# Moving one operand sum behind two masks, half of a normalising to VectorE, two loads ahead of three stores, and one bias step to a later slice

## The chip, the core and the metric

The kernel runs on one core of a Trainium2 chip. The core has five instruction queues that matter here: TensorE (PE; its weight loads are listed apart as PEld), VectorE (DVE), ScalarE (ACT), GpSimd (POOL) and SyncE (SP), which in this kernel only issues DMAs. Each queue runs its instructions strictly in the order in which they were written; queues wait for each other through semaphores. The metric is the device time of one execution in microseconds, as the median of several runs; less is better.

## The reference

`x` is 128 graphs of 128 nodes with 768 features, `adj` a weighted adjacency matrix for each graph, and there are 12 heads of 64 features. All numbers are float32.

```python
h = jnp.maximum(_layernorm(x, axis=-1), 0.0)
q, k, v = (_split_heads(h @ W + b) for W, b in ((Wq, bq), (Wk, bk), (Wv, bv)))
scores = jnp.einsum('bhqd,bhkd->bhqk', q, k) / jnp.sqrt(HD)
scores = scores + beta * adj_e
scores = jnp.where(adj_e > 0, scores, -9000000000000000.0)
out = jnp.einsum('bhqk,bhkd->bhqd', softmax(scores, axis=-1), v)
x = x + merge_heads(out)
```

## The kernel before

The 128 graphs are worked in 32 groups of four (G = 0 to 31). For each group the hidden rows `h` are turned so that features lie on the partitions (tiles A00 to A12), and three projections follow, called slices: "qk0" (heads 0 to 5 of Q and K), "v" (V), and "qk1" (heads 6 to 11 of Q and K). Behind every slice some of the attention is woven in: `scores` (Q against K on TensorE into a PSUM buffer), a mask (one VectorE instruction, line 637, which adds the bias and so frees that PSUM buffer), the exponential on ScalarE (line 639), and `attend` (line 686).

Group 0 is computed by `plain_slice`: ordinary tiled matmuls (line 845), 18 steps a slice. Groups 1 to 31 are computed by `slice_z`: a slice is 15 products (table PRODUCTS), each the matmul of a sum of activation tiles (S0 to S14, or an A tile itself) with a sum of weight tiles (T...). A product is 14 matmuls of line 550, which the profile counts as 28 because a float32 matmul has two records. The 15 products are spread over four chains a, b, c, d; the products of a chain add up in one PSUM buffer, and after each product VectorE (line 574) or ScalarE (lines 568 and 570, for the first use of an output tile) takes the buffer's present state into the output tiles (`home`). So a chain's next product waits for the eviction of its last one. There are four PSUM buffers in all (`pairs`), for chains, scores and attention together.

The order of the 15 products in a slice is written out: PORDER for "qk0" and "v", QORDER for "qk1", ZORDER for "qk0" of group 1 alone, LORDER for the last slice. I call the first product of a slice place 0 and the last place 14. In PORDER places 0 to 9 hold products 1, 0, 5, 2, 3, 10, 7, 6, 13, 11; their chains are a, c, a, c, b, a, b, c, a, b. In ZORDER product 7 stands at place 5.

What else is done at a place is hung into `todo`. `run` takes a product's matmuls, then the masks that are pending, then `todo[at]`, then what is overdue, then the product's evictions, then what trails, and then `todo[at, "post"]`. From the end of the first slice on this order is kept as written on every engine (`manual_schedule`).

- Activation sums are VectorE instructions of line 467 on 128x896 elements (`sum_acts`). In "qk0" S7 stands at place 0, S0 at 1, S5 at 5, S14 at 8, S11 at 9; for group 1 S6 stands ahead of S7. S7 is A01 - S10 and is read by product 7 and by the sum S14; S0 is read by product 10.
- At place 2 of "qk0" two scores are issued, so their masks (tiles e_5 and e_3) come behind the product at place 3. For group 1 these scores stand at places 3 and 5. A third score follows place 6.
- Most weight sums are kept in DRAM and streamed in (`load_T`, line 338; tile T_qk or T_v) into a ring of five buffers; 11 of the 45 stay resident. A product that used a streamed one issues the next load.
- The weight sums are made once, during group 0, by `prepare`: `sums` and `rest` (lines 303, 305, 282, 283 on VectorE, 285 to 288 on GpSimd) and a store to DRAM (`kept`, line 291). The steps are taken one or two at a place; the last stores and the first five loads of group 1 fall into group 0's "qk1" slice, the loads at places 10 to 14.
- Group 0's rows 2 and 3 of `x` are normalised in place: `moments_2` makes the scale (line 395) and the shift (line 397) on GpSimd, `norm` applies them in four ScalarE instructions a graph (line 449), and `to_hT` turns them on VectorE (line 462).
- `halve_bias` (line 977) is one GpSimd instruction that turns the V bias into the form that `slice_z` wants; it stands at place 1 of group 0's "qk1", and its result is first read in group 1's "v".

Of the kernel before, what the change touches and what calls it, by code (L numbers as in the profile page):

```python
# [14 lines left out]
ALU = mybir.AluOpType  # L15
# [4 lines left out]
GRP = 4  # L20
# [89 lines left out]
QORDER = (4, 0, 1, 8, 2, 3, 5, 6, 7, 10, 9, 11, 13, 12, 14)  # L110
LORDER = (1, 4, 0, 8, 5, 2, 10, 3, 6, 7, 13, 9, 11, 12, 14)
PORDER = (1, 0, 5, 2, 3, 10, 7, 6, 13, 11, 4, 9, 14, 8, 12)
ORDER = {"qk0": PORDER, "v": PORDER, "qk1": QORDER}
RING = 5
RESIDENT = (3, 8, 12, 16, 20, 25, 29, 33, 35, 38, 41)

# [10 lines left out]
def direct(ctx, tc, x, adj, wq, bq, wk, bk, wv, bv, beta, out, bad):  # L127
# [10 lines left out]
    nc = tc.nc  # L138
# [10 lines left out]
    NB = P // SQ  # L149
# [12 lines left out]
    xg, xp, A, full, wide, biasT, vt, qk = {}, {}, {}, {}, {}, {}, {}, {}  # L162
# [7 lines left out]
    def block(i):  # L170
        return flat(7 * P * i, 7 * P * (i + 1)).rearrange("p (z n) -> p z n", n=P)
# [22 lines left out]
    for g in range(2):  # L194
        t = xg[0, g]
# [64 lines left out]

    sequence = [(sl, n) for sl in ("qk0", "v", "qk1") for n in ORDER[sl]]
    resident = {key: const.tile([P, 7, P], F32, name=f"res_{key[0]}_{key[1]}") for key in (sequence[at] for at in RESIDENT)}
# [3 lines left out]
    def quarters(t):  # L266
        return t[:, 0:6].rearrange("p (c z) n -> p c z n", c=2)[:, :, 0:2]

    def prepare(sl):

        def home(name):
            n = [i for i, p in enumerate(PRODUCTS) if p[1] == name][0]
            if (sl, n) in resident:
                return resident[sl, n]
            made_in[0] += sl != "qk1"
            if sl != "qk1" and made_in[0] % 8 in (2, 5, 7):
                t = work.tile([P, 2, W], F32, tag="e", name=f"prep_{sl}_{n}", bufs=3)
                return t.rearrange("p i w -> p (i w)")[:, 0:7 * P].rearrange("p (z n) -> p z n", n=P)
            return work.tile([P, 7, P], F32, tag="T", name=f"prep_{sl}_{n}", bufs=RING)

        def rest(n, t, b11, b12, b22, b=None):
            nc.vector.tensor_tensor(t[:, 6], b12, b11, ALU.subtract)
            nc.vector.tensor_tensor(t[:, 2], b22, b12, ALU.add)
            if b is not None:
                nc.gpsimd.tensor_copy(t[:, 0:2], b[:, 0])
                nc.gpsimd.tensor_copy(t[:, 3], b[:, 1, 0])
            nc.gpsimd.tensor_tensor(t[:, 4], t[:, 1], t[:, 6], ALU.add)
            nc.gpsimd.tensor_tensor(t[:, 5], t[:, 0], t[:, 4], ALU.subtract)
            if (sl, n) not in resident:
                k = kept[sl, n] = dram.tile([P, 7, P], F32, name=f"kept_{sl}_{n}")  # L290
                nc.sync.dma_start(k, t)

        made = {}

        def sums(name):
            for out, a, b, sign in SUMS_B:
                if out == name:
                    if out not in made:
                        made[out] = home(out)
                    at = [quarters(made[q]) if q in made else wt[sl, q] for q in (a.strip("-"), b)]  # L300
                    op = ALU.add if sign > 0 else ALU.subtract
                    if a[0] == "-":
                        nc.vector.scalar_tensor_tensor(quarters(made[out]), at[0], -1.0, at[1], op0=ALU.mult, op1=op)
                    else:
                        nc.vector.tensor_tensor(quarters(made[out]), at[0], at[1], op)

        def finish(name):
            n = [i for i, p in enumerate(PRODUCTS) if p[1] == name][0]
            if name in made:
                t = made[name]  # L310
                rest(n, t, t[:, 3], t[:, 4], t[:, 1])
            else:
                t, b = home(name), wt[sl, name]
                rest(n, t, b[:, 1, 0], b[:, 1, 1], b[:, 0, 1], b)

        steps = []
        for first, then_finish in PREPARED:
            for name in first:
                steps.append(lambda name=name: sums(name))
            for name in then_finish:  # L320
                steps.append(lambda name=name: finish(name))
        return steps

    def order_of(G, sl):
        if G == 1 and sl == "qk0":
            return ZORDER
        return LORDER if G == NG - 1 and sl == "qk1" else ORDER[sl]

# [27 lines left out]
    st, pm, rstd, shift = {}, {}, {}, {}  # L356
# [88 lines left out]
    def norm(G, g, lo=0, hi=NB):  # L445
        for b in range(lo, hi):
            t = xg[G, g][:, b, :]
            n = g * NB + b
            nc.scalar.activation(t, t, AF.Relu, bias=shift[G, n], scale=rstd[G, n])  # L449

    def home_A(G, name):
        if (G, name) in wide:
# [11 lines left out]
    def sum_acts(G, name):  # L464
        _, a, b, sign = [row for row in SUMS_A if row[0] == name][0]
        t = full[G, name] = block(SPOT.index(name))
        nc.vector.tensor_tensor(t, full[G, a], full[G, b], ALU.add if sign > 0 else ALU.subtract)  # L467
# [411 lines left out]
    first = {}  # L879
# [71 lines left out]
    def half(step):  # L951

        if step == 0:
            for g in range(2, GRP):
                stats(0, g)
        elif step == 1:
            first["got"] = moments_1(0, 2 * NB, 4 * NB)
        else:
            first["pool"] = moments_2(0, 2 * NB, 4 * NB, *first["got"])
            for g in range(2, GRP):  # L960
                norm(0, g)
            for k in range(3):
                first["dve"] = to_hT(0, 1, k)

# [17 lines left out]
    todo, steps, mom = {}, {}, []  # L982

    def then(at, f, *args):
        todo.setdefault(at, []).append(lambda: f(*args))

    def bias(G, *at):
        def go():
            if G not in steps:
                steps[G] = bias_steps(G)  # L990
            next(steps[G], None)
        for n in at:
            then(n, go)
# [17 lines left out]
    def sums_at(G, slots):  # L1011
        for at, name in slots:
            then(at, sum_acts, G, name)
# [43 lines left out]
    turn_act(1, ((4, "A01"), (5, "A02"), (6, "A00"), (9, "A10"), (10, "A11"), (11, "A12")))  # L1057
    for n in range(18):
        then(n, step, 2 - (n > 8))
    then(1, halve_bias)  # L1060
    sums_at(1, ((12, "S1"), (13, "S9"), (14, "S10"), (15, "S2")))
    then(0, row_moments, 2)
    then((7, "post"), load_x, 2, 0)
    then((14, "post"), load_row, 3, 0)
    then(12, homes.append, block(len(SPOT)))
    bias(1, 4, 6, 8)
    for n in range(RING):
        then(10 + n, load_T)
    plain_slice(0, "qk1", todo, (1, 0))

    for G in range(1, NG):
        more = G + 1 < NG
        todo.clear()
        then(2 + (G == 1), scores, G - 1, 1, 2)
        then(2 + 3 * (G == 1), scores, G - 1, 1, 0)
        then((6, "post"), scores, G - 1, 1, 1)
        attention(G - 1, 1, ((7, 2), (10, 0), (12, 1)))
        sums_at(G, ((0, "S7"), (1, "S0"), (5, "S5"), (8, "S14"), (9, "S11")))
        if G == 1:
            todo[0].insert(0, lambda: sum_acts(1, "S6"))  # L1080
        if more:
            for n, at in enumerate((1, 2, 4, 5)):
                then((at, "post"), norm, G + 1, n // 2, n % 2 * 2, n % 2 * 2 + 2)
            turn_act(G + 1, ((8, "A01"), (9, "A00"), (11, "A02")), None)
            then((12, "post"), load_x, G + 1, 1)
            if G + 2 < NG:
                then((7, "post"), row_stats, G + 2, 0)
                then((9, "post"), load_row, G + 2, 1)
        slice_z(G, "qk0", todo)

        todo.clear()
        then(2, scores, G, 0, 2)
        then(2, scores, G, 0, 1)
        then(7, scores, G, 0, 0)
        if more:
            then((11, "post"), add_raw, G + 1)
            for n, at in enumerate((3, 4, 6, 7)):
                then((at, "post"), norm, G + 1, 2 + n // 2, n % 2 * 2, n % 2 * 2 + 2)
            turn_act(G + 1, ((10, "A11"),), 1)
            for at, name in ((4, "A01"), (5, "A00"), (6, "A02")):  # L1100
                then(at, inner, G + 1, name)
            if G + 2 < NG:
                for g, at in ((1, 1), (2, 5), (3, 10)):
                    then((at, "post"), row_stats, G + 2, g)
                    if g < 3:
                        then((at + 1, "post"), load_row, G + 2, g + 1)
        slice_z(G, "v", todo)

        todo.clear()
        if not more:  # L1110
            break
        attention(G, 0, ((3, 2), (9, 1)))
        attention(G, 0, ((12, 0),), 6)
        turn_act(G + 1, ((1, "A10"), (4, "A12")), 1)
        sums_at(G + 1, ((6, "S1"), (7, "S9"), (8, "S2"), (11, "S6"), (13, "S10")))
        bias(G + 1, 0, 2, 4)
        if G + 2 < NG:
            then(5, row_moments, G + 2, 6, 9)
            then((6, "post"), load_x, G + 2, 0)
        if G + 3 < NG:  # L1120
            then((10, "post"), load_row, G + 3, 0)
        slice_z(G, "qk1", todo)
# [158 lines left out]
```

## Time and profile before

| | |
|---|---|
| median of 3 runs | 2697.48 us (2691.35 to 2700.34) |
| the profiled execution's own time | 2692.31 us |
| its span, first to last instruction | 2690.5 us |
| mean granted TensorE clock | 0.997 |
| one middle group (912.15 to 993.60 us) | 81.45 us, of which PE busy 81.17, PEld 79.43, DVE 67.32, POOL 66.00, ACT 55.48; DMA share 0.89 |
| group 0 and the way to group 1's first product (0 to 126.9 us) | PE busy 32.61 of the first 40, 48.00 of the next 48, 37.54 of the last 38.9 |

Times are microseconds from the start of the span. A timeline row has the start, the time, the engine, the line, the operation, the tiles written and read, the shape and a count; in brackets stands the idle time of that engine before it and what ended it. A row of the waits has the waiting engine and line, what it waited for, the total, the number of times and the longest. The profile's matmul ends are modelled and overlap, so idle time of TensorE is read from the weight loads (PEld) and from the distance of starts.

### The profile page before, as it was taken

How to read it: one execution, taken by the hardware profiler on the slowest of the kernel's cores; microseconds unless marked ns; L12 is line 12 of the kernel's file. 1: busy time of each engine (PE TensorE's matmuls, PEld its weight loads, DVE VectorE, ACT ScalarE, POOL GpSimd, SP SyncE). 2: the span in 40 equal slices, each digit the busy share in tenths (PEclk: the TensorE clock that was granted, in tenths of full speed). 3: DMA queues.
4: the chain of work that ended last, by engine and by line, in shares of the span. 5: the costliest groups of instructions: out<-in, count | busy, mean ns of one | idle time of the engine just before them, and what ended most of it. 6: DMA issues, size and time to landing. Idle time of an engine off the chain costs nothing.

```text
span 2690.5 us, 121410 instructions
## 1 busy us (share of the span) xinstructions
PE 2650.9 (99%) x52029; PEld 2564.3 (95%) x52029; DVE 2185.2 (81%) x2705; ACT 1751.2 (65%) x4612; POOL 2111.8 (78%) x3034
## 2 busy tenths in 40 slices
PE   8999999999999999999999999999999999999997
PEld 7799999999999999999999999999999999999997
DVE  6878888878888788888788877788887888887886
ACT  2576766677666677666766666776667676667553
POOL 4867878877888778788778787787887787887783
PEclk9999999999999999999999999999999999999999
DMA  9889888989889898889898888888898988898875
GB/s 228 275 258 280 276 273 271 275 277 272 270 268 286 262 285 274 272 275 281 264 279 279 264 272 271 271 279 271 278 273 267 278 283 270 272 284 268 257 238 155
DMA packets 530341, 721.71 MB, mean 268 GB/s; under 512 B 105980, under 2 KB 374024, under 8 KB 529800
## 3 DMA queue, kind: packets, MB, share of 16 engines
q1 hardware_dynamic: 528640, 713.12, 85.9%
q8 instruction: 411, 6.73, 1.0%
q10 hardware_dynamic: 1160, 0.79, 0.2%
q14 instruction: 130, 1.06, 0.1%
HBM read 647.73 MB, written 66.05 MB: 265 GB/s over the span
## 4 chain that ended last, share of the span: by engine, by line
PE 77%; DVE 13%; DMA 3%; issue 2%; POOL 1%; ACT 0%; SPq 0%; POOLq 0%; DVEq 0%; ACTq 0%
PE pair L550 67%; PE pair L686 5%; PE pair L629 5%; DVE home L574 4%; DVE sbig L467 3%; DVE e L637 1%; DMA T_qk<-kept_qk 1%; DMA T_v<-kept_v 1%; DMA out_dram<-xo 1%; DVE xo L711 1%; DVE home L595 1%; DVE home L593 1%; DVE home L592 1%; DVE sbig L574 0%; DVE home L594 0%
## 5 line engine op out<-in xcount | busy, mean ns | idle before, releaser
L574 DVE TENSOR_TENSOR home<-home,pair 128x896 f32<-128x896 f32 x810 | 860.9, 1076 | 276.0 <-PE pair L550 236.9
L550 PE MATMUL pair<-sbig,T_qk 128*64 128x128 f32 x13020 | 827.8, 273 | 9.7 <-DVE e L637 7.3
L550 PEld LDWEIGHTS pair<-sbig,T_qk 128*64 128x64 f32 x13020 | 708.0, 137 | 20.9 <-DVE e L637 14.0
L550 PE MATMUL pair<-A,T_qk 128*64 128x128 f32 x6944 | 463.7, 273 | 0.0
L669 ACT ACTIVATE e<-e,sm 128x64 f32<-128x64 f32 x1512 | 382.0, 343 | 111.7 <-DVE sm L657 111.5
L592 POOL TENSOR_TENSOR home<-home 128x256 f32<-128x256 f32 x297 | 265.8, 895 | 226.2 <-DVE home L574 222.2
L550 PE MATMUL pair<-T_v,sbig 128*64 128x128 f32 x6944 | 418.3, 274 | 5.5 <-issue 2.8
L686 PE MATMUL pair<-v,e 128*64 128x65 f32 x6048 | 401.8, 221 | 0.5 <-DVE e L637 0.5
L550 PEld LDWEIGHTS pair<-T_v,sbig 128*64 128x64 f32 x6944 | 381.5, 137 | 20.1 <-issue 17.4
L568 ACT ACTIVATE home<-pair 128x640 f32<-128x640 f32 x325 | 231.2, 711 | 260.3 <-PE pair L550 200.0
L550 PEld LDWEIGHTS pair<-A,T_qk 128*64 128x64 f32 x6944 | 378.1, 137 | 5.9 <-issue 5.5
L686 PEld LDWEIGHTS pair<-v,e 128*64 128x64 f32 x6048 | 359.8, 137 | 3.9 <-DVE e L637 1.0
L550 PE MATMUL pair<-sbig,res_qk 128*64 128x128 f32 x4340 | 288.5, 273 | 0.0
L593 POOL TENSOR_TENSOR home<-home 128x256 f32<-128x256 f32 x297 | 248.4, 836 | 23.3
L595 POOL TENSOR_TENSOR home<-home 128x256 f32<-128x256 f32 x297 | 240.3, 809 | 23.3
L550 PEld LDWEIGHTS pair<-sbig,res_qk 128*64 128x64 f32 x4340 | 234.6, 137 | 5.3 <-issue 5.3
L695 ACT ACTIVATE sm<-pair,tiny 128x8 f32<-128x8 f32 x189 | 49.3, 261 | 286.9 <-PE pair L686 286.9
L594 POOL TENSOR_TENSOR home<-home 128x128 f32<-128x128 f32 x297 | 213.9, 720 | 23.3
L449 ACT ACTIVATE x<-x,block 128x192 f32<-128x192 f32 x480 | 231.8, 553 | 0.0
L637 DVE SCALAR_TENSOR_TENSOR e<-pair,biasT 128x1024 f32<-128x1024 f32 x189 | 225.0, 1216 | 3.2 <-PE pair L629 3.2
L639 ACT ACTIVATE e<-e 128x1024 f32<-128x1024 f32 x189 | 193.7, 1065 | 47.0 <-DVE e L637 39.1
L472 POOL TENSOR_TENSOR A<-A 128x256 f32<-128x256 f32 x186 | 169.9, 914 | 59.2 <-DVE A L462 59.2
(197 smaller groups left out, 4604.3 us busy)
## 6 DMA issues: line engine op xcount, KB each, us to landing
T_qk<-kept_qk SPq DMA_DIRECT2D x713, 448.0 KB, 4.9
T_v<-kept_v SPq DMA_DIRECT2D x341, 448.0 KB, 4.7
xo<-in_x_dram SPq DMA_DIRECT2D x189, 256.0 KB, 4.4
out_dram<-xo SPq DMA_DIRECT2D x189, 256.0 KB, 6.0
x<-in_x_dram SPq DMA_DIRECT2D x248, 192.0 KB, 6.7
sbig<-in_x_dram SPq DMA_DIRECT2D x116, 384.0 KB, 6.3
kept_qk<-prep_qk SPq DMA_DIRECT2D x23, 448.0 KB, 2.9
adj<-in_adj_dram SPq DMA_DIRECT2D x128, 64.0 KB, 4.5
```

The lines of the kernel that those rows point to most:

```text
L449: nc.scalar.activation(t, t, AF.Relu, bias=shift[G, n], scale=rstd[G, n])
L550: nc.tensor.matmul(p[q:q + HD, at, :], lhs[:, q:q + HD], rhs, start=(first and at % 4 == 0), stop=True, skip_group_check=True)
L568: nc.scalar.activation(t[:, 0:5], p[:, 0:5], AF.Copy, scale=float(sign))
L574: nc.vector.tensor_tensor(t, t, p[:, 0:7], op)
L592: e.tensor_tensor(t[:, 1:4:2], t[:, 1:4:2], twice(5), ALU.add)
L593: e.tensor_tensor(t[:, 2:5:2], t[:, 2:5:2], twice(1), ALU.add)
L594: e.tensor_tensor(t[:, 4], t[:, 4], t[:, 6], ALU.add)
L595: e.tensor_tensor(t[:, 0:7:6], t[:, 0:7:6], twice(2), ALU.add)
L637: nc.vector.scalar_tensor_tensor(e, ps, SCORE_CAP * ISCALE, bias, op0=ALU.min, op1=ALU.add)
L639: trailing.append(lambda: nc.scalar.activation(e, e, AF.Exp, scale=1.0 / ISCALE))
L669: nc.scalar.activation(o[:, r, b, 0:HD], pa[:, r, b, 0:HD], AF.Copy, scale=t[:, 1, r, b:b + 1])
L686: nc.tensor.matmul(pa[q:q + HD, 2 * g + i, :], k[:, q:q + HD], vt[G, "v", r, h // 4][:, 4 * g + h % 4, :], start=True, stop=True, skip_gro ...
```

## The change

- A new order XORDER for "qk0" of groups 2 to 31: products 7 and 6 change places (6 and 7), all else as PORDER.
- In "qk0" of groups 1 to 31, S7 is no longer summed at place 0 but behind place 4 ("post"), and S0 at place 0 instead of 1. For group 1, whose order stays ZORDER, S7 then stands directly ahead of product 7 at place 5.
- Group 0, rows of graph 2: four VectorE instructions with the scale and shift as per-partition scalars and one VectorE maximum with zero over the whole graph, instead of four ScalarE instructions. Graph 3 stays on ScalarE.
- The first two of group 1's streamed loads become steps of the preparation, between the sums T0, T6, T1, T10 and the finishing and storing of T6, T1, T0. All later preparation steps move back by the two steps that this takes.
- `halve_bias` goes from group 0's "qk1" to place 4 of group 1's "qk0".

```diff
-ORDER = {"qk0": PORDER, "v": PORDER, "qk1": QORDER}
+XORDER = (1, 0, 5, 2, 3, 10, 6, 7, 13, 11, 4, 9, 14, 8, 12)
+ORDER = {"qk0": XORDER, "v": PORDER, "qk1": QORDER}
...
         for first, then_finish in PREPARED:
             for name in first:
                 steps.append(lambda name=name: sums(name))
+            if sl == "qk1" and first[0] == "T0":
+                steps += [load_T, load_T]
             for name in then_finish:
...
+    def norm_dve(G, g):
+        for b in range(NB):
+            t = xg[G, g][:, b, :]
+            n = g * NB + b
+            nc.vector.tensor_scalar(t, t, rstd[G, n], shift[G, n], op0=ALU.mult, op1=ALU.add)
+        t = xg[G, g]
+        nc.vector.tensor_scalar(t, t, 0.0, None, op0=ALU.max)
...
-            for g in range(2, GRP):
-                norm(0, g)
+            norm_dve(0, 2)
+            norm(0, 3)
...
-    then(1, halve_bias)
...
-    for n in range(RING):
+    for n in range(2, RING):
         then(10 + n, load_T)
...
-        sums_at(G, ((0, "S7"), (1, "S0"), (5, "S5"), (8, "S14"), (9, "S11")))
+        sums_at(G, ((0, "S0"), ((4, "post"), "S7"), (5, "S5"), (8, "S14"), (9, "S11")))
         if G == 1:
             todo[0].insert(0, lambda: sum_acts(1, "S6"))
+            then(4, halve_bias)
```

## The prediction

> **What bounds the kernel now.** I read the page first, then the totals of the waits, then one middle group as a timeline, engine by engine, and last the way from group 0 to group 1.
>
> ```profile
> PE 2650.9 (99%) x52029; PEld 2564.3 (95%) x52029; DVE 2185.2 (81%) x2705; ACT 1751.2 (65%) x4612; POOL 2111.8 (78%) x3034
> ...
> PE 77%; DVE 13%; DMA 3%; issue 2%; POOL 1%; ACT 0%; SPq 0%; POOLq 0%; DVEq 0%; ACTq 0%
> ```
>
> TensorE sets the time. Its matmuls cover 99% of the span and its weight loads 95%, so only a few per cent can be won without taking matmuls away, and the change takes none away. The chain of waits has 13% on VectorE, though, so somewhere TensorE stands behind it. The totals of TensorE's waits say where:
>
> ```profile
> PEld pair L550 <- DVE e L637: 14.7, 29, 0.7
> ...
> PE pair L550 <- DMA T_qk<-kept_qk: 2.4, 5, 0.9
> PE pair L550 <- DMA T_v<-kept_v: 2.2, 2, 1.8
> ```
>
> The first row is one wait of 0.5 us (14.7 / 29) in nearly each of the 31 groups of products. What waits is a product; what ends it is a mask. In a middle group it looks so, first TensorE, then VectorE:
>
> ```profile
> 955.21 1.51 PEld L550 LDWEIGHTS pair<-sbig,res_qk 128*64 128x64 f32 x28 [0.17 <-issue]
> 957.23 4.57 PEld L550 LDWEIGHTS pair<-sbig,T_qk 128*64 128x64 f32 x84 [0.52 <-DVE e L637]
> ...
> 963.00 1.75 PE L550 MATMUL pair<-A,T_qk 128*64 128x128 f32 x28
> ...
> 964.58 0.39 PE L550 MATMUL pair<-sbig,res_qk 128*64 128x128 f32 x4
> ...
> 967.04 3.23 PE L550 MATMUL pair<-A,T_qk 128*64 128x128 f32 x56
> ```
>
> ```profile
> 952.36 1.07 DVE L574 TENSOR_TENSOR home<-home,pair 128x896 f32<-128x896 f32 x1
> 953.36 1.42 DVE L467 TENSOR_TENSOR sbig<-A,sbig 128x896 f32<-128x896 f32 x1
> 954.70 1.34 DVE L467 TENSOR_TENSOR sbig<-sbig 128x896 f32<-128x896 f32 x1
> 955.97 2.34 DVE L637 SCALAR_TENSOR_TENSOR e<-pair,biasT 128x1024 f32<-128x1024 f32 x2
> 958.23 0.97 DVE L711 TENSOR_TENSOR xo<-xo,e 128x512 f32<-128x512 f32 x1
> 959.13 1.08 DVE L574 TENSOR_TENSOR home<-home,pair 128x896 f32<-128x896 f32 x1
> 960.13 1.08 DVE L467 TENSOR_TENSOR sbig<-A,sbig 128x896 f32<-128x896 f32 x1
> 962.19 1.09 DVE L574 TENSOR_TENSOR home<-home,pair 128x896 f32<-128x896 f32 x1 [0.98 <-PE pair L550]
> 963.19 1.22 DVE L637 SCALAR_TENSOR_TENSOR e<-pair,biasT 128x1024 f32<-128x1024 f32 x1
> 964.87 1.09 DVE L574 TENSOR_TENSOR home<-home,pair 128x896 f32<-128x896 f32 x1 [0.46 <-PE pair L550]
> ```
>
> The 28 loads from 955.21 are place 3; place 4 opens chain b and needs a free PSUM buffer, which the first mask (955.97 to about 957.15) gives back. It would have begun at 956.72 and begins at 957.23. VectorE is without a break from 952.36 to 961.2, so the mask is late because of what stands before it: S7 (953.36) and S0 (954.70).
>
> **The steady part of the change.** S7 leaves the front: the next instruction came 1.34 us after it (953.36 to 954.70), so the masks begin about 1.3 us sooner, the first at 954.65, ending at 955.85. Its scores were issued from 953.3 and are not in its way (both scores fit before 955.21). TensorE wants the buffer at 956.72; the wait goes with 0.85 us to spare. I take all of it: 29 x 0.51 = **14.7 us**. It can't give more, since the wait is then nil; it gives less only if something else is late.
>
> What is late next? S7 is read by product 7, which XORDER puts at place 7. Behind the masks VectorE has: `xo` to 957.6, the eviction of place 4 (TensorE ends it near 958.3; from TensorE's next start to an eviction it is 964.87 less 964.58, 0.3 us) to 959.7, S7 to 960.7, S5 to 961.7. Place 7 begins at 963.00 less the 0.5 us won, 962.5: 1.8 us to spare for S7. Without the exchange product 7 would stand at place 6, from 959.7, and wait for S7; so the exchange is what makes the move free. Its own price: chain b's products are now at places 4, 7 and 9 rather than 4, 6 and 9, so the eviction of product 7 must be done within place 8. It follows the third mask as the eviction at 964.87 does now, so it runs from about 964.4 to 965.4, and place 9 begins at 967.04 less 0.5, 966.5: 1.1 us to spare. Chain c (places 3, 6, 11 instead of 3, 7, 11) is evicted at place 3 by ScalarE; I find nothing late there. VectorE's idle time at 962.19 (0.98) and 964.87 (0.46) pays for the 1.1 us of S7. Bounds for this part: 14.7 won; 0 if another wait stands right behind.
>
> **Group 0: the normalising.** Rows of POOL, ACT, DVE and PE:
>
> ```profile
> 28.19 0.20 POOL L397 TENSOR_TENSOR shift<-mean,rstd 128x8 f32<-128x8 f32 x1
> ...
> 28.92 0.40 POOL L285 COPY prep_qk<-sbig 128x256 f32<-128x256 f32 x1
> ...
> 28.43 3.61 ACT L449 ACTIVATE x<-x,shift,rstd 128x192 f32<-128x192 f32 x8 [3.12 <-POOL shift L397]
> 32.08 1.90 DVE L462 STREAM_TRANSPOSE A<-x 128x512 f32<-128x512 f32 x3 [5.71 <-ACT x L449]
> ...
> 32.84 15.81 PE L845 MATMUL pair<-A,sbig 128*128 128x256 f32 x72 [1.53 <-DVE A L462]
> ...
> L910 DVE TENSOR_SCALAR rows<-sbig,mvrow,rsrow 128x256 f32<-128x256 f32 x6 | 2.1, 410 | 0.7 <-POOL rsrow L900 0.7
> ...
> L493 DVE TENSOR_SCALAR adj<-biasT 128x512 f32<-128x512 f32 x32 | 13.9, 434 | 11.7 <-ACT adj L491 11.7
> ```
>
> Eight ScalarE instructions take 3.61 us while VectorE waits. Four are left, 1.8 us, to 30.25. Beside them VectorE does five that no row shows in this shape. Each of the four (192 elements) takes no more than the 410 ns for 256 elements with the same kind of scalars, and no less than half; the maximum over 768 lies between the 434 ns for 512 and 1.5 times that. So 1.3 to 2.3 us; I take 1.8, nearest the first row scaled down (0.31 each), and it ends with ScalarE's at 30.3. The transposes start 1.8 us sooner and TensorE's 1.53 us of waiting go. Bounds: 1.53, and 0 if the new instructions must wait out the copies that GpSimd does beside them (one of them is quoted; they end near 30.1, after which 1.8 us lead back to 32). The preparation behind the transposes moves forward by the same.
>
> The Trainium skill has a rule against this ("SBUF — State Buffer", section "Who interferes with whom"): VectorE in a two-port mode and GpSimd hold a shared port pair in turn, for whole instructions. By it the copies and the new instructions take turns, and if these lost every turn the 1.5 us would be nothing, the lower bound above; no run here shows which side waits.
>
> **Group 0 to group 1.** Three small waits of TensorE lie here:
>
> ```profile
> 96.45 1.45 POOL L977 TENSOR_TENSOR bv_b<-bv_b 128x384 f32<-128x384 f32 x1
> ...
> 112.90 0.54 DVE L282 TENSOR_TENSOR prep_qk<-prep_qk 128x128 f32<-128x128 f32 x1
> ...
> 114.49 1.21 DVE L637 SCALAR_TENSOR_TENSOR e<-pair,biasT 128x1024 f32<-128x1024 f32 x1
> ...
> 115.75 0.31 PEld L686 LDWEIGHTS pair<-v,e 128*64 128x64 f32 x8 [0.96 <-DVE e L637]
> ...
> 126.90 1.54 PEld L550 LDWEIGHTS pair<-sbig,T_qk 128*64 128x64 f32 x28 [1.31 <-issue]
> ...
> 128.85 4.59 PEld L550 LDWEIGHTS pair<-sbig,T_qk 128*64 128x64 f32 x84 [0.42 <-issue]
> ```
>
> The mask at 114.49 comes ahead of four small instructions, since the two load steps push the finishing of T1 and T0 behind it: 112.90 to 114.49, 1.6 us sooner, so 0.96 goes. The loads of products 1 and 0 are issued at place 6 or 7 instead of behind all stores, so 1.31 + 0.42 can go. The stores, the group's `x` load and two `xo` loads stand behind them on SP; the third load stays where it was. `halve_bias` (1.45 us) leaves a crowded GpSimd and lands in an idle one:
>
> ```profile
> 132.53 1.19 POOL L288 TENSOR_TENSOR res_qk<-res_qk 128x128 f32<-128x128 f32 x1
> 144.86 1.51 POOL L592 TENSOR_TENSOR home<-home 128x256 f32<-128x256 f32 x1 [11.14 <-DVE home L574]
> ...
> 132.06 1.34 DVE L467 TENSOR_TENSOR sbig<-sbig 128x896 f32<-128x896 f32 x1
> ...
> 136.92 1.07 DVE L467 TENSOR_TENSOR sbig<-A,sbig 128x896 f32<-128x896 f32 x1
> ...
> 136.24 1.70 PE L550 MATMUL pair<-sbig,T_qk 128*64 128x128 f32 x28
> ```
>
> 11.14 us of idle time hide it; without that cover it would cost its 1.45 once. The one new wait: group 1 keeps product 7 at place 5 (136.24), and S7 now follows the mask that ended near 136.9. Without S7 in front (1.3) and with S7 behind (1.0) it is ready near 136.7 on today's clock, so product 7 would wait 0.4 us, and more for each us that TensorE comes sooner than VectorE. So of 1.53 + 0.96 + 1.73 = 4.2 us not all arrives: behind product 7 the time is VectorE's, which the earlier normalising, the emptier GpSimd and the reordering bring forward by some 1.5 to 3. I take **2.0 us** for the whole start; bounds -0.5 (only the new wait) and 4.2.
>
> **The sum.** 14.7 + 2.0 = 16.7 us, less 1 us since the streamed loads (rows of T_qk and T_v above, 4.6 us of waits in all) meet a slightly quicker TensorE: 15.7. The profiled execution took 2692.3, so one like it takes 2676.6. The median of the runs shown lies 5.2 above it, at 2697.5, which gives 2681.8. I name **2681**.
>
> **Rivals.**
> (1) *Another wait stands behind the mask*, and half or more of the 0.5 us comes back at a streamed load. For it: DMA is nearly full in just this stretch:
>
> ```profile
> 938.00:957.00 19.00, 18.96 (x404) 18.29 (x398) 18.78 (x21) 10.17 (x33) 17.82 (x22) 1.00 1.01 322
> ```
>
> (the last three are clock, DMA share and GB/s). Against it: TensorE's waits for streamed loads are seven in the whole run. With 7 us left of the 14.7 and 1 of the start: 2697.5 - 8, 2689.5.
> (2) *The change doesn't do what it says*: the mask isn't what holds place 4, since the last of a wait's several causes is all that the profile names, and nothing is won in the groups; 0 to 2 us at the start, 2696. Against it: the mask's end and the load at 957.23 lie within 0.1 us.
> (3) *Slower.* Product 7's eviction doesn't fit within place 8. From the 1.1 us of slack each further us of delay on VectorE is a wait of the same length at place 9, in 30 groups; a delay of 2.1 us costs 30 x 1.0 against the 15.7: 2697.5 + 14.3, 2712. It decides from 1.6 us of delay on (30 x 0.5). Against it: VectorE idles 1.44 us in that stretch.
>
> **How the numbers follow.** Forecast 0.70, rival 1 0.13, rival 2 0.08, rival 3 0.09. The forecast's own range is 2673 to 2689 (start from -0.5 to 4.2, and 5 us either way for runs that spread over 9 us). 0.3% is 8.1 us, about what a measurement can tell: faster means below 2689.4. Faster: nearly all of the forecast and half of rival 1, 0.75. Same: the rest of both and most of rival 2, 0.16. Slower 0.09. The range goes to 2694 to take in rival 1, and down to 2671.
>
> **What would show it.** Right: the row "PEld pair L550 <- DVE e L637" falls from 14.7 to under 2; a middle group takes 80.95 instead of 81.45 us; S7 stands behind two masks and no wait at product 7 or at place 9 appears; the transposes of group 0 begin near 30.3; the first product of group 1 doesn't wait for its load. Wrong: a new row of TensorE waiting for line 574 or 467 with some 30 times (rival 3), or for T_qk and T_v with far more than seven (rival 1).

## The result and the profile after

The changed kernel takes 2687.32 us (median of 7 runs, 2684.84 to 2690.76). The kernel before, on the same chip, takes 2694.63 (7 runs, 2691.35 to 2700.34). The ratio is 0.9975, 95% interval 0.9966 to 0.9985: 7.3 us less, where the prediction had 16 (2697 to 2681). The time lies within the predicted range, which was wide enough to hold rival 1 too, and it lies nearer to the 2681 named than the gain does to the 16 by luck: the prediction started from 2697.48 us, the median of three runs of the kernel before, and over seven runs that kernel came out 2.9 us lower. The profiled execution took 2687.3 us, 5.0 less than the one before.

Lines of the changed kernel stand 11 further down in the parts that matter: the products are line 561 (550 before), VectorE's evictions 585 (574), ScalarE's 579 and 581 (568, 570), the masks 648 (637), the exponentials 650 (639), `attend` 697 (686), the sums 478 (467). Line 708 is ScalarE's copy of what `attend` left in PSUM, which gives that buffer back.

From the page of the changed kernel, the busy times and the chain of waits by engine:

```profile
PE 2651.8 (99%) x52029; PEld 2561.9 (95%) x52029; DVE 2180.8 (81%) x2710; ACT 1747.4 (65%) x4608; POOL 2062.7 (77%) x3034
...
PE 42%; POOL 30%; ACT 14%; issue 6%; DMA 4%; DVE 3%; SPq 0%; ACTq 0%; POOLq 0%; DVEq 0%
```

The shares of busy time hardly differ from those before. The chain does: VectorE fell from 13% to 3%, and ScalarE, which had 0%, has 14%. (GpSimd's 30% comes and goes with it, as a later chain shows.) Something that runs over ScalarE now sets the end. The waits of TensorE's weight loads in the changed kernel, and one of VectorE's (total, times, longest):

```profile
PEld pair L697 <- DVE e L648: 13.0, 29, 0.5
PEld pair L561 <- ACT e L708: 4.9, 28, 0.4
...
PEld pair L561 <- DVE sbig L478: 1.8, 1, 1.8
...
DVE home L585 <- ACT home L581: 18.6, 24, 0.8
```

The row in which a product waited for a mask 29 times is gone. In its place `attend` waits for a mask 29 times, 0.45 us each, and a product waits 28 times for ScalarE to give a buffer back. VectorE's adds to an output tile wait 24 times, 0.78 us each, for ScalarE's write to one, which is not in VectorE's list before. The wait has moved, and not to the streamed loads. The middle group from 861.61 to 943.13, by the view of windows (length, then busy time of PE, PEld, DVE, ACT and POOL):

```profile
861.61:943.13 81.52, 81.31 (x1649) 79.41 (x1647) 67.07 (x80) 55.41 (x146) 64.49 (x95) 1.00 0.89 275
```

81.52 us, against 81.45 before and 80.95 forecast; the mean over the 29 groups from 2 to 30 is 81.84, against 81.83 before. Where within the group the time went is seen from the distance between the first weight loads of neighbouring places of "qk0", as a mean over groups 2 to 30:

| place | before | after | difference |
|---|---|---|---|
| 3 | 1.98 | 1.47 | -0.51 |
| 4 | 1.48 | 1.53 | +0.05 |
| 8 | 2.51 | 2.94 | +0.43 |
| 9 | 1.48 | 1.68 | +0.20 |
| 10 | 1.53 | 1.48 | -0.05 |

All of the 0.51 us is won at place 3, as forecast, and all of it is given back five and six places later. The timeline of a middle group of the changed kernel shows how, first TensorE's weight loads:

```profile
951.36 3.09 PEld L561 LDWEIGHTS pair<-sbig,T_qk 128*64 128x64 f32 x56
954.42 1.56 PEld L561 LDWEIGHTS pair<-A,T_qk 128*64 128x64 f32 x28
...
957.19 1.51 PEld L561 LDWEIGHTS pair<-sbig,T_qk 128*64 128x64 f32 x28 [0.17 <-issue]
958.66 0.25 PEld L561 LDWEIGHTS pair<-sbig,res_qk 128*64 128x64 f32 x4
959.37 0.31 PEld L697 LDWEIGHTS pair<-v,e 128*64 128x64 f32 x8 [0.46 <-DVE e L648]
...
963.56 1.51 PEld L561 LDWEIGHTS pair<-A,T_qk 128*64 128x64 f32 x28 [0.43 <-ACT e L708]
```

The 56 loads from 951.36 are places 4 and 5 without a break; place 6 is product 6 (954.42), place 7 is product 7 (957.19), place 8 begins at 958.66, and there the attention that is woven into it stops for 0.46 us. The last row is place 10, which waits for the copy of line 708. VectorE in the same stretch:

```profile
949.39 2.34 DVE L648 SCALAR_TENSOR_TENSOR e<-pair,biasT 128x1024 f32<-128x1024 f32 x2
...
953.22 1.09 DVE L585 TENSOR_TENSOR home<-home,pair 128x896 f32<-128x896 f32 x1 [0.58 <-PE pair L561]
954.22 2.09 DVE L478 TENSOR_TENSOR sbig<-A,sbig 128x896 f32<-128x896 f32 x2
957.10 1.09 DVE L585 TENSOR_TENSOR home<-home,pair 128x896 f32<-128x896 f32 x1 [0.79 <-ACT home L581]
958.10 1.22 DVE L648 SCALAR_TENSOR_TENSOR e<-pair,biasT 128x1024 f32<-128x1024 f32 x1
959.24 1.08 DVE L585 TENSOR_TENSOR home<-home,pair 128x896 f32<-128x896 f32 x1
```

S7 and S5 (954.22) are done in time, at 956.3. Then VectorE stands idle for 0.79 us with work at hand: the add of product 6 (957.10) waits for ScalarE. The third mask stands behind that add in the queue and ends at 959.3; the `attend` at 959.37 takes the PSUM buffer that this mask gives back. ScalarE, the changed kernel and then the kernel before:

```profile
948.04 0.69 ACT L579 ACTIVATE home<-pair 128x640 f32<-128x640 f32 x1
...
953.04 2.04 ACT L650 ACTIVATE e<-e 128x1024 f32<-128x1024 f32 x2
954.94 1.02 ACT L452 ACTIVATE x<-x,block 128x192 f32<-128x192 f32 x2
955.81 0.74 ACT L579 ACTIVATE home<-pair 128x640 f32<-128x640 f32 x1
956.40 0.67 ACT L581 ACTIVATE home<-pair,bqk 128x128 f32<-128x128 f32 x2
```

```profile
953.36 0.69 ACT L568 ACTIVATE home<-pair 128x640 f32<-128x640 f32 x1
...
958.36 2.04 ACT L639 ACTIVATE e<-e 128x1024 f32<-128x1024 f32 x2
960.26 1.02 ACT L449 ACTIVATE x<-x,block 128x192 f32<-128x192 f32 x2
961.13 0.73 ACT L568 ACTIVATE home<-pair 128x640 f32<-128x640 f32 x1
```

Product 10 at place 5 is the first product that adds to the output tile (0,2), so ScalarE copies it (955.81 to 957.1). Product 6 is the second use of the same tile, so VectorE's add has to follow that copy. Before, product 7 stood between the two and gave ScalarE a whole place more. And ScalarE doesn't come sooner: from its copy of product 0 (place 1) to the one of product 10 (place 5) it takes 955.81 - 948.04 = 7.77 us after and 961.13 - 953.36 = 7.77 us before. The windows of this stretch, after and before, show why:

```profile
948.04:957.93 9.89, 9.89 (x224) 9.38 (x224) 8.52 (x9) 9.89 (x23) 5.33 (x7) 1.00 0.74 214
```

```profile
953.36:963.25 9.89, 9.61 (x214) 8.86 (x214) 8.91 (x10) 9.89 (x23) 6.05 (x7) 1.00 0.72 216
```

The fourth busy time is ScalarE's: 23 instructions in 9.89 us of 9.89, in both. An engine that is busy 65% of the span is full here, and TensorE, 0.5 us ahead, runs into it.

**The start.** Between the two profiles group 2 begins 5.06 us earlier (210.87 and 205.81), and the 29 groups from there to group 31 take 2373.0 us before and 2373.3 after: the whole difference of the two profiles lies ahead of group 2. Some 2.0 us of it are not the change's: the instruction that makes the scale begins at 26.44 us before and 24.42 after. TensorE's granted clock differed ahead of it, as the windows from 10.5 to 16 us show, before and after (the last three numbers are clock, DMA share and GB/s):

```profile
10.50:16.00 5.50, 5.12 (x30) 5.00 (x30) 1.05 (x4) 1.16 (x5) 0.44 (x2) 0.69 0.72 188
```

```profile
10.50:16.00 5.50, 5.46 (x46) 5.20 (x47) 0.69 (x3) 1.48 (x6) 0.64 (x3) 1.00 0.77 194
```

From the scale to group 2 it is 184.43 us before and 181.39 after, 3.0 us less. The way to group 1's first product has 2.7 of them (100.46 and 97.74; 97.0 to 97.4 in the six other kernels with the same start), group 1's "qk0" gives 1.2 back (30.08 and 31.31), and its "v" has 1.4 (27.99 and 26.61). That last part can't be put down to the change: in the twelve profiles group 1's "v" takes from 26.2 to 30.5 us. So about 1.5 us are the change's. Group 0 of the changed kernel, VectorE, GpSimd and TensorE's loads:

```profile
26.41 1.41 DVE L458 TENSOR_SCALAR x<-x,rstd,shift 128x192 f32<-128x192 f32 x4 [2.07 <-POOL shift L400]
27.85 0.64 DVE L460 TENSOR_SCALAR x<-x 128x768 f32<-128x768 f32 x1
28.59 1.90 DVE L473 STREAM_TRANSPOSE A<-x 128x512 f32<-128x512 f32 x3
...
26.56 0.49 POOL L286 COPY res_qk<-sbig 128x256 f32<-128x256 f32 x1
...
28.02 0.61 POOL L287 COPY prep_qk<-sbig 128x128 f32<-128x128 f32 x1
...
29.36 15.41 PEld L856 LDWEIGHTS pair<-A,sbig 128*128 128x128 f32 x72 [0.47 <-DVE A L473]
```

The five VectorE instructions take 1.41 + 0.64 = 2.05 us, and of TensorE's wait 0.47 us are left (1.93 before, in the weight loads).

### The profile page after: what moved, and what is told of

It reads as the page before. It is cut to its first block, busy times and chain, and to the rows that moved or that the text cites. A ratio compares the mean times of both kernels' runs of the same rounds, so it can differ in the third digit from the quotient of the medians.

```text
span 2685.5 us, 121474 instructions
## 1 busy us (share of the span) xinstructions
PE 2651.8 (99%) x52029; PEld 2561.9 (95%) x52029; DVE 2180.8 (81%) x2710; ACT 1747.4 (65%) x4608; POOL 2062.7 (77%) x3034
## 4 chain that ended last, share of the span: by engine, by line
PE 42%; POOL 30%; ACT 14%; issue 6%; DMA 4%; DVE 3%; SPq 0%; ACTq 0%; POOLq 0%; DVEq 0%
PE pair L561 32%; POOL v L618 4%; PE pair L697 4%; PE pair L856 3%; POOL v L617 3%; POOL A L483 3%; POOL home L616 3%; PE pair L640 3%; ACT x L452 3%; ACT e L650 3%; ACT home L581 2%; ACT home L579 2%; POOL home L603 2%; POOL home L605 2%; POOL v L614 2%
## 5 line engine op out<-in xcount | busy, mean ns | idle before, releaser
L561 PEld LDWEIGHTS pair<-sbig,T_qk 128*64 128x64 f32 x13020 | 707.6, 137 | 12.1 <-issue 6.7
L603 POOL TENSOR_TENSOR home<-home 128x256 f32<-128x256 f32 x297 | 245.0, 825 | 270.7 <-DVE home L585 252.0
L606 POOL TENSOR_TENSOR home<-home 128x256 f32<-128x256 f32 x297 | 238.5, 803 | 23.3
L604 POOL TENSOR_TENSOR home<-home 128x256 f32<-128x256 f32 x297 | 229.2, 772 | 23.3
```

The lines of the kernel that those rows point to most:

```text
L561: nc.tensor.matmul(p[q:q + HD, at, :], lhs[:, q:q + HD], rhs, start=(first and at % 4 == 0), stop=True, skip_group_check=True)
L603: e.tensor_tensor(t[:, 1:4:2], t[:, 1:4:2], twice(5), ALU.add)
L604: e.tensor_tensor(t[:, 2:5:2], t[:, 2:5:2], twice(1), ALU.add)
L606: e.tensor_tensor(t[:, 0:7:6], t[:, 0:7:6], twice(2), ALU.add)
```

## The experiments

Of "before on the same chip" there are 23 runs for the first four kernels (2693.12 us) and 15 for the next three (2691.64).

**The parts alone.** e1_start_only has all of the change in groups 0 and 1 but keeps the order and the sums of the kernel before. e2_sum_only is the kernel before with the new order and the new place of S7 and nothing else.

```diff
# e1_start_only, against the changed kernel
-ORDER = {"qk0": XORDER, "v": PORDER, "qk1": QORDER}
+ORDER = {"qk0": PORDER, "v": PORDER, "qk1": QORDER}
...
-        sums_at(G, ((0, "S0"), ((4, "post"), "S7"), (5, "S5"), (8, "S14"), (9, "S11")))
+        sums_at(G, ((0, "S7"), (1, "S0"), (5, "S5"), (8, "S14"), (9, "S11")))
```

> The changed kernel with the old order of the products and S7 and S0 back in front of the masks; the normalising, the two loads and the bias step stay changed. Theory (the groups gained nothing, the whole 7 us came from the start): as fast as the changed kernel or up to 2 us faster, because group 1 no longer waits for S7: 2685 to 2688, group 2 begins near 204 to 206 us instead of 210.9, the 0.5 us wait for the mask is back in some 29 groups (row of 14 to 15 us). Rival (the groups gained and the start's part is chance): like the kernel before, 2693 to 2696, group 2 begins near 210.

```diff
# e2_sum_only, against the kernel before
+XORDER = (1, 0, 5, 2, 3, 10, 6, 7, 13, 11, 4, 9, 14, 8, 12)
+ORDER = {"qk0": XORDER, "v": PORDER, "qk1": QORDER}
...
-        sums_at(G, ((0, "S7"), (1, "S0"), (5, "S5"), (8, "S14"), (9, "S11")))
+        sums_at(G, ((0, "S0"), ((4, "post"), "S7"), (5, "S5"), (8, "S14"), (9, "S11")))
```

> The kernel before with the new order and the moved sums alone. Theory: nothing won in the groups, the wait of 0.5 us goes from place 4 and comes back as about 0.45 us at place 8 and 0.2 at place 10, and group 1 waits some 2 us for S7: 2694 to 2698, no faster than before. Rival (the groups gained, the start's part is chance): 5 to 8 us faster than before.

e1: 2689.45 us (12 runs), ratio 0.9990 (0.9981 to 0.9998), 3.7 us less than before. e2: 2690.55 us (11 runs), ratio 0.9990 (0.9982 to 0.9999), 2.6 us less. The waits of TensorE in e1, where the mask's old wait is still there, and then in e2, where the two new ones stand already:

```profile
PEld pair L561 <- DVE e L648: 15.3, 29, 0.6
```

```profile
PEld pair L687 <- DVE e L638: 12.6, 29, 0.5
PEld pair L551 <- ACT e L698: 4.3, 28, 0.2
```

So the moved sum and the exchange by themselves make the new waits (in e2's lines, 687 is `attend` and 638 the mask). Of the 7.3 us about half is the start's (3.7, by e1's interval 0.5 to 5.1). e2's own 2.6 us (0.3 to 4.8) are not to be seen in its profile, where its 29 groups take 2374.0 us, 1.0 more than before, and what it gained stays open.

**ScalarE's order.** e3_exp_later is the changed kernel, but in "qk0" of groups 2 and later what trails behind places 3 and 4 (the two exponentials) is held back until behind place 5, so that ScalarE's copy of product 10 comes ahead of them. e4_ten_before_three leaves ScalarE's order alone and puts product 10 one place sooner instead, so that two places lie between the first and the second use of tile (0,2).

```diff
# e3_exp_later, against the changed kernel
-    def run(products, todo):
+    def run(products, todo, hold=()):
...
-            trail()
+            if at not in hold:
+                trail()
...
-        run([product_z(G, sl, n) for n in order_of(G, sl)], todo)
+        run([product_z(G, sl, n) for n in order_of(G, sl)], todo, (3, 4) if sl == "qk0" and G > 1 else ())
```

> The changed kernel, but in the first Q/K slice of groups 2 to 31 what trails behind places 3 and 4 (the two exponentials on ScalarE) waits until place 5 has been evicted. Theory (product 6's eviction on VectorE waits 0.8 us for ScalarE, which is late with place 5's copy because of the two exponentials, and so the third mask and the attention behind it are late): the 0.8 us wait of VectorE goes, the third mask ends some 0.8 us sooner, the 0.45 us of place 8 go nearly whole and the 0.2 us of place 10 with them: 12 to 18 us faster than the changed kernel, 2670 to 2676. Rival (VectorE is simply full behind the masks, S7's 1.05 us make the third mask late whatever ScalarE does): no faster than 2685, the wait at place 8 stays at 0.4 us.

```diff
# e4_ten_before_three, against the changed kernel
-XORDER = (1, 0, 5, 2, 3, 10, 6, 7, 13, 11, 4, 9, 14, 8, 12)
+XORDER = (1, 0, 5, 2, 10, 3, 6, 7, 13, 11, 4, 9, 14, 8, 12)
```

> The changed kernel with products 10 and 3 exchanged (places 4 and 5), so that the first and second writing of one output tile lie two places apart and the PSUM buffer that the first mask frees is wanted one place later. Theory (ScalarE's late copy is the cause): the wait at place 8 goes, 10 to 18 us faster than the changed kernel, unless product 10 at place 4 now waits for ScalarE's eviction of chain a from place 2 (then up to 0.3 us a group come back, 9 us). Rival (VectorE is simply full): the third mask is no sooner, 2685 to 2689, wait at place 8 still 0.4 us.

e3: 2674.80 us (6 runs), ratio to the kernel before 0.9934 (0.9915 to 0.9953). e4: 2677.31 us (5 runs), ratio 0.9942 (0.9929 to 0.9956). Both intervals lie wholly below that of the changed kernel (0.9966 to 0.9985). The 29 waits of `attend` for a mask are in neither's list; a product waits for line 708 not once in e3 and twice, 0.4 us in all, in e4; VectorE's 18.6 us of waiting for ScalarE's write are 0.6 in e3 and 1.1 in e4. A middle group of e3 by windows, its chain of waits, and then ScalarE, VectorE and TensorE's loads in a middle group of e3:

```profile
1102.65:1183.59 80.94, 80.94 (x1648) 79.44 (x1646) 67.21 (x80) 55.59 (x146) 63.62 (x95) 1.00 0.90 278
...
PE 96%; POOL 1%; DVE 1%; DMA 1%; issue 1%; ACT 0%; ACTq 0%; SPq 0%; POOLq 0%; DVEq 0%
...
951.81 0.70 ACT L579 ACTIVATE home<-pair 128x640 f32<-128x640 f32 x1 [0.68 <-PE pair L561]
952.41 0.62 ACT L581 ACTIVATE home<-pair,bqk 128x128 f32<-128x128 f32 x2
952.90 2.01 ACT L650 ACTIVATE e<-e 128x1024 f32<-128x1024 f32 x2
...
951.28 2.09 DVE L478 TENSOR_TENSOR sbig<-A,sbig 128x896 f32<-128x896 f32 x2
953.39 1.09 DVE L585 TENSOR_TENSOR home<-home,pair 128x896 f32<-128x896 f32 x1
954.40 1.22 DVE L648 SCALAR_TENSOR_TENSOR e<-pair,biasT 128x1024 f32<-128x1024 f32 x1
...
955.72 0.25 PEld L561 LDWEIGHTS pair<-sbig,res_qk 128*64 128x64 f32 x4
955.94 0.37 PEld L697 LDWEIGHTS pair<-v,e 128*64 128x64 f32 x8
```

Now ScalarE waits 0.68 us for TensorE at that copy, no longer the other way round. VectorE goes from the sums to the add of product 6 without a break, the third mask ends near 955.6, and `attend` at 955.94 waits for nothing. This group takes 80.94 us, what the prediction had named, and TensorE has 96% of the chain. It is one of the shortest: the mean over the 29 groups is 81.53 us, against 81.83 before, since "qk0" is 0.46 us shorter a group and "v" 0.15 us longer. VectorE does the same work as in the changed kernel, so it was not simply full; it stood behind ScalarE. This version beats both kernels.

**Are both conditions needed?** e6_order_only keeps the exchange and the start but puts S7 and S0 back in front. e7_sum_old_order keeps S7 behind place 4 but undoes the exchange.

```diff
# e6_order_only, against the changed kernel
-        sums_at(G, ((0, "S0"), ((4, "post"), "S7"), (5, "S5"), (8, "S14"), (9, "S11")))
+        sums_at(G, ((0, "S7"), (1, "S0"), (5, "S5"), (8, "S14"), (9, "S11")))
# e7_sum_old_order, against the changed kernel
-ORDER = {"qk0": XORDER, "v": PORDER, "qk1": QORDER}
+ORDER = {"qk0": PORDER, "v": PORDER, "qk1": QORDER}
```

> The changed kernel with the new order kept, S7 and S0 back in front of the masks. Theory (products 10 and 6 back to back on one output tile make VectorE wait for ScalarE): the 0.5 us wait at place 4 is back, and the order by itself brings some 0.3 to 0.4 us more a group at places 8 to 10: 9 to 14 us slower than with both old (2689.5), 2698 to 2704. Rival (the order is harmless, the late S7 fills VectorE): as with both old, 2688 to 2691, nothing at places 8 to 10.

> The changed kernel with the old order, S7 summed behind place 4 as in the change. Theory (product 7 at place 6 must now wait for S7, which ends near 1.0 us after place 6 could begin; the 0.5 us at place 4 go): 0.4 to 0.7 us a group more than with both old, 2700 to 2710, a row of TensorE waiting for line 478 with some 30 times and 25 to 35 us. Rival (S7 is done in time, the exchange wasn't needed): 2672 to 2680.

e6: 2690.84 us (11 runs), ratio 0.9997 (0.9988 to 1.0006). e7: 2705.40 us (5 runs), ratio 1.0053 (1.0039 to 1.0067). The rows of e6, TensorE's waits and VectorE's timeline, and the one of e7's waits:

```profile
PEld pair L561 <- DVE e L648: 15.4, 29, 0.6
...
961.17 1.09 DVE L585 TENSOR_TENSOR home<-home,pair 128x896 f32<-128x896 f32 x1 [1.27 <-ACT home L581]
962.17 1.22 DVE L648 SCALAR_TENSOR_TENSOR e<-pair,biasT 128x1024 f32<-128x1024 f32 x1
```

```profile
PEld pair L561 <- DVE sbig L478: 28.0, 31, 0.9
```

e6 came out better than I had expected, with a time in the rival's range: VectorE's wait for ScalarE is there, and even longer (1.27 us), yet places 8 and 9 take only 2.54 and 1.60 us, 0.15 more than before. TensorE still loses its 0.5 us at place 4 and is not ahead of ScalarE. So the exchange alone costs little, and the 0.43 us at place 8 need both: the two uses of a tile back to back (in e4, without them, place 8 takes 2.52 us), and a TensorE that arrives 0.5 us sooner. That VectorE is full behind the late S7, as e6's rival has it, is what e3 and e4 speak against. e7 shows the exchange to be necessary, as the prediction said: without it product 7 waits 0.9 us (28.0 / 31) for S7 in every group, and the kernel is slower than before by 13.8 us.

**Group 1's own wait.** e5_later_and_first is e3 with S7 of group 1 back at place 0, since product 7 of group 1 waits 1.8 us for it once (the third row of the changed kernel's waits).

```diff
# e5_later_and_first, against e3_exp_later
-        sums_at(G, ((0, "S0"), ((4, "post"), "S7"), (5, "S5"), (8, "S14"), (9, "S11")))
+        early = ((0, "S7"), (1, "S0")) if G == 1 else ((0, "S0"), ((4, "post"), "S7"))
+        sums_at(G, early + ((5, "S5"), (8, "S14"), (9, "S11")))
```

> The run before last's version (exponentials behind place 5's eviction), and S7 of group 1 alone back at place 0. Theory (group 1's wait for S7 is 1.5 to 1.8 us, since its product 7 stands at place 5): 1 to 2 us faster than without, 2672 to 2674, the row of TensorE waiting for line 478 (1.8 us) gone. Rival (the earlier S7 only delays group 1's other sums and masks by as much): no difference within 1 us.

2676.31 us (5 runs), ratio 0.9943 (0.9929 to 0.9956): no gain over e3 that can be told. The wait moved once more. Places 4 to 6 of group 1 take 3.33 + 2.71 + 2.71 = 8.75 us in e3 and 1.55 + 2.77 + 3.73 = 8.05 in e5, where the score behind place 6 now waits for a mask. Of 1.8 us 0.7 are won, too little to be seen.

**The three parts of the start, one run each**, all against the kernel before: e8_norm_only has the normalising alone, e9_loads_only the two load steps, e10_bias_only the moved bias step.

```diff
# e8_norm_only
-            for g in range(2, GRP):
-                norm(0, g)
+            norm_dve(0, 2)
+            norm(0, 3)
# e9_loads_only
+            if sl == "qk1" and first[0] == "T0":
+                steps += [load_T, load_T]
...
-    for n in range(RING):
+    for n in range(2, RING):
# e10_bias_only
-    then(1, halve_bias)
...
+            then(4, halve_bias)
```

> The kernel before with the normalising of graph 2 on VectorE alone. Theory (each of the three small parts takes its own wait away): TensorE's 1.53 us wait for the transposes is gone, the transposes begin some 2.2 us behind the end of the shift instead of 3.7; the waits at the last mask of group 0 (0.96) and at group 1's first two loads (1.31 and 0.42) stay. From the start of the scale instruction to group 1's first product: 99 us instead of 100.5. Rival (the start is limited by the preparation on VectorE and GpSimd, which only moves along): 100 to 101, the time comes back as longer waits before group 1.

> The kernel before with the two loads put ahead of the last three stores alone. Theory: the 1.53 us wait stays; the waits for the last mask (0.96) and for the first two loads (1.31 and 0.42) go. From the start of the scale instruction to group 1's first product 97.5 to 98.5 us instead of 100.5. Rival: the stores behind the loads come so much later that the third load is late by as much; 99.5 to 100.5 and a wait at group 1's third product.

> The kernel before with the bias step moved alone. Theory: 1.45 us off GpSimd's queue in group 0 bring VectorE's preparation forward by at most that, the 0.96 us wait for the last mask shrinks to nothing, the loads' waits stay; 99.5 to 100.5 us from the scale instruction to group 1's first product; nothing new in group 1. Rival: it changes nothing, 100.5, the 0.96 stays.

They took 2694.35, 2689.11 and 2693.92 us beside 2695.03 for the kernel before, one run each, which by itself decides nothing. Their traces show where the waits went. In e8 TensorE's wait for group 0's transposes is 0.48 us instead of 1.93; the last mask's 0.96 is gone there too, but group 1's first product then waits 2.40 us instead of 1.31. In e9 no wait is left between 108 and 130 us: the last mask's 0.96 and the loads' 1.31 and 0.42 are gone. In e10 the mask's 0.96 is gone as well, and the first two products still wait 0.38 and 1.01. So each of the three edits is enough for the 0.96 us, and the change, which has all of them, wins it once. From the scale to group 1's first product the three take 99.36, 98.50 and 98.80 us, against 100.46 before: 1.1, 2.0 and 1.7 us less, e10 more than expected. All three together win 2.7 us there in the changed kernel and 3.4 in e1, less than the sum of the parts.

## Why the prediction was right about the wait and wrong about what comes behind it

- **The wait for the first mask** (14.7 us). Right: it is gone in all 29 groups, and place 3 is 0.51 us shorter.
- **S7 in time, the eviction of product 7 in time.** Right: S7 is done at 956.3 and product 7's first load is at 957.19, 0.9 us later (1.8 was forecast). No place waits for product 7's eviction, so rival 3 didn't happen.
- **"What is late next?"** This step failed. The prediction followed VectorE's queue and TensorE's products, took the third mask to follow as it did before, and closed with "Chain c ... is evicted at place 3 by ScalarE; I find nothing late there". Two links were missed. First, it asked who writes the PSUM buffers and not who writes the output tile: products 10 and 6 are the first and second use of tile (0,2), and the exchange sets them side by side, so that VectorE's add waits 0.79 us for ScalarE's copy. Of ScalarE's load in the groups the prediction has only its 65% of the span, and ScalarE is full for 9.89 us just there. Secondly, the `attend` at place 8 takes the buffer that the third mask frees. TensorE's loads in the kernel before:

```profile
964.70 0.37 PEld L686 LDWEIGHTS pair<-v,e 128*64 128x64 f32 x8
```

  Before, the mask (963.19 and 1.22 us long) ended at 964.41 and the `attend` began at 964.70. After, 0.05 us lie between the two (959.32 and 959.37) where the `attend` waits, so the mask had about 0.24 us to spare, against a TensorE that came 0.5 us sooner. In the profiles the 14.7 us became about nothing: 29 x (-0.51 + 0.05 + 0.43 + 0.20 - 0.05) = 3.5 us lost at these places, 3.2 in the whole of "qk0", and 2.7 us won in "v" (2.5 of them at its places 2 to 4, which take 10.8 us more than their shortest lengths before and 8.3 after); 0.3 us more in all. By e2's runs 2.6 us (0.3 to 4.8) of the 14.7 were won.
- **Rival 1** has the time (2689.5) and the kind, another wait behind the one removed; its place, a streamed load, is wrong for the change: the excess at places 2 to 4 of "v" is 2.5 us smaller. Against this rival the prediction had seven waits, 4.6 us in all. Those are the ones that the profile ascribes to a load by name; the excess at these three places alone was 10.8 us.
- **The start** (2.0 us). About right: 2.7 us on the way to group 1's first product less 1.2 us in its "qk0" is 1.5 us in the profiles; by e1's runs, which keep S7 of group 1 in front, 3.7 us. The VectorE normalising took 2.05 us where 1.8 was taken (1.3 to 2.3), and won 1.93 - 0.47 = 1.46 us of TensorE's waiting, where 1.53 was the upper bound. The wait of 0.96 and those of the loads went. `halve_bias` was hidden. Product 7 of group 1 waits 1.8 us for S7, where at least 0.4 was forecast.
- **The size that was meant.** With ScalarE's order mended (e3) the kernel takes 18.3 us less than before by the same chip's runs (12.7 to 22.9 by the interval), where the prediction had 16 for the change. In the profiles "qk0" of the 29 groups is 13.4 us shorter than before, of the 14.7 forecast, while "v" is 4.2 us longer, where the prediction took off 1 us for the streamed loads. The missed links cost what lies between e3 and the changed kernel, about 11 us by the ratios (0.9975 less 0.9934, of 2694.6), 9.0 us over the 29 groups of the profiles.

What stays open: the excess at places 2 to 4 of "v" sums to between 7.5 and 18.2 us in the profiles of these kernels (8.3 in the changed kernel, 14.1 in e3, 18.2 in e5, but also 18.0 in e7, the slowest). Most of it lies ahead of products that use a streamed load, though the profile names the load at few of them. I could not tie it to TensorE's pace, and didn't try it by itself.

## What to carry to other kernels

When a wait is taken away, follow each buffer and each output tile of the next few places to its last writer and its next user, on every engine, and look how much slack each had against an engine that comes sooner by the whole gain. An engine's share of the span says nothing of a stretch: take its busy time in a window around the change, and where it is full there, its work stays where it is while the others move ahead. Two instructions of different engines on the same tile belong at least as far apart as the slower engine is behind; here one place more was enough (e4).

## What the runs showed of the hardware

- The start varies by itself, with the clock that TensorE is granted. In seven of the twelve profiles the granted clock was 0.5 for 3.41 or 6.83 us, beginning between 9.6 and 12.1 us; there 24 matmuls of group 0 took 4.3 to 5.5 us, and the instruction that makes the scale, which waits for statistics that TensorE sums behind them, began at 25.4 to 27.7 us. In the other five the clock stayed at 1.0, the 24 matmuls took 2.95 us, and the scale began at 24.1 to 24.4. The first instruction that reads these rows of `x` began at 18.5 to 19.2 us in all twelve, so the load of `x` is not the reason. Kernels with the same start are on both sides (e1 and e3), so it is not the change either. Two profiles of the start are compared from an anchor behind such a stretch, not from zero; otherwise 2 of the 5 us between the two would have been put down to the change.
- VectorE beside GpSimd: while VectorE ran its five new instructions, GpSimd's copies of 128x256 took 0.42 to 0.49 us instead of 0.40, and one of 128x128 took 0.61 where its like took 0.29 to 0.31. The Trainium skill ("SBUF — State Buffer", section "Who interferes with whom") has the two hold a shared port pair in turn when VectorE is in a two-port mode. The trace doesn't show in which mode VectorE ran, so whether this is that rule stays open; what it shows is that GpSimd's six copies took 0.5 us more in all. The five VectorE instructions took 2.05 us, within the bounds of 1.3 to 2.3, so they did not wait out the copies.
